# Input statistics of all images taken in the first attention, and new tables for the scan

## The chip, the core and the metric

The kernel runs on one core of a Trainium2 chip. The metric is the device time of one execution in microseconds (us). The core has engines that run their own instruction streams in order and wait for each other on semaphores: TensorE (PE, matmuls and, as PEld, the loads of their weights), VectorE (DVE), ScalarE (ACT), GpSimd (POOL), and SyncE (SP), whose queue issues all the transfers that this document speaks of. Data lies in HBM, in SBUF (on chip, 128 partitions) and in PSUM (where matmuls write).

## What is computed

The input x has 8 images of 256 channels and 48 x 48 = 2304 positions. Two layers are added to it in turn, each behind a group norm (32 groups of 8 channels, so statistics over a whole image are needed before anything else):

```python
def _L0_conv_ref(x, W, bias):          # attention over positions
    tokens = x.reshape(b, c, n).transpose(0, 2, 1)
    feat_pos = tokens @ W.T + bias
    feat, pos = feat_pos[:, :, :c], feat_pos[:, :, c:]
    pos = pos / jnp.maximum(jnp.linalg.norm(pos, axis=-1, keepdims=True), 1e-12)
    sim = jnp.einsum('bnc,bmc->bnm', pos, pos)
    topksim, topkid = jax.lax.top_k(sim, K)            # K = 16
    out = softmax(topksim) weighted sum of feat[topkid]

def step(h, inp):                      # state-space layer, twice in depth
    dA = jnp.exp(dt_t[:, :, None] * A)
    h = h * dA + dt_t[:, :, None] * B_t[:, None, :] * x_t[:, :, None]
    y = jnp.einsum('bds,bs->bd', h, C_t)

x = x + _L0_conv_ref(_gn(x), ...)
x = x + _L1_conv_ref(_gn(x), ...)
```

The second layer is a scan over the 2304 positions with 512 inner channels and 16 states, with a layer norm, an input projection, a convolution of four taps, softplus, a gate (silu of z) and an output projection around it, and all that twice (depth 2).

## The kernel before, in words

**The scan** is the long part. Positions are cut into 6 chunks of T = 384, and each chunk and depth of an image is a *unit*: 12 units an image, 96 in all. A unit has 16 *steps* (32 inner channels with 4 groups of states on 128 partitions, 4 states in each row), and a step has two *parts* of two states each. So a unit has 32 parts and an image 384. The main loop at the end runs over the parts `m` and writes out the order of every engine's work by hand (`manual_schedule`). In each part:

- `decay` on ACT: exp(dt A) for the next part, into one of two PSUM banks (L871);
- `run_scan` on DVE: the scan of the part (L886). `SHARE` says by a letter for each part who multiplies the result by C: with V, DVE does so at once (L888, and ACT's `carry` saves the last column); with G, POOL does it later for the step (`pool_part`, L914), in one instruction of 1536 columns where both parts of the step are G, of 768 where one is;
- at a step's first part, `make_bx` on POOL: the product of B and dt x for a step two ahead (L847), into one of 8 buffers;
- the rows of the tables `between` (ahead of the scan) and `behind` (after it) that fall on this part: loads, projections, norms, `sum_states` (PE sums the states of four steps, L932, and frees their bx buffers), `gate` (DVE, L938), `out_proj` (PE) and `leave` (L967, the residual, DVE; or L963, ACT). A row is (part, function, arguments). Its part counts from the unit's first part, and is negative where it prepares the unit during the one before, so parts over 31 lie in the next unit;
- one step of the generator `layer0` (`ahead.go`).

**The attention** of the first image runs alone before the scan, in pools of its own, under a scheduler that orders the instructions. The attention of image b + 1 runs beside the scan of image b. `layer0` first takes the statistics of the image (`input_stats`, L247: six chunks loaded, bn_stats on DVE, then `group_stats`, a few small operations on DVE, PE, ACT and POOL in turn); then it prepares (`chunk`, `normalized`, `scale`: normalize on ACT, project on PE, norms of pos); then it goes through 18 row blocks of 128 positions, one every 16 parts, by the table `within`: similarities (PE, `similar`; ACT, `keep_similar`), the 16 largest (DVE, `top`, four passes over 2304 columns, L466 to L473), the weights (`others`, `turn`, `weights`), their sum (`weigh`, L516), and the residual (`turn_back`, `finish`, L541), where `average` loads x for one block of 128 positions, `finish` adds and takes bn_stats for the next group norm (L543), and stores x1. `PHASE` and `BLOCK` let the blocks start only at one part in 16.

`layer0` of the first image also takes the statistics of image 1 during its row blocks, one step in every fourth part. For images 2 to 7 the statistics are taken beside the scan, as soon as the image before is done (`Ahead.turn`); in the parts of an image's scan this is from part -42. `SHARE` has three strings: units 1 to 9 of images 0 to 6, which have row blocks beside them; units 0, 10 and 11 of these; and the last image. The tables have two sets: with blocks, and without (`between_spare`, `behind_spare`, chosen by `beside_none`).

Of the kernel before, what the change touches and what calls it, by code (L numbers as in the profile page):

```python
# [1 line left out]

# [13 lines left out]
P = 128  # L16
# [9 lines left out]
def tile_conv_preact(  # L26
# [27 lines left out]
    T = 384  # L54
# [16 lines left out]
    EARLY = -24  # L71
# [3 lines left out]
        "GGVGGGVVGGGGGGVGGGVVGGGVGGGGGVVG",  # L75
        "GVGGVGVVGVVVGVGVGGGGVGVVGVGVGVGV",
        "VGVGVGVGVGVVGGGVGGGVVGVVGVVGGGVG",
# [106 lines left out]
    def group_stats(st, found, mm0, name, more=None):  # L184
# [23 lines left out]
        rstd = small.tile([P, CB], F32, tag="gn_rstd", name=f"rstd_{name}", bufs=4)  # L208
# [5 lines left out]
        shift = small.tile([P, CB], F32, tag="gn_shift", name=f"shift_{name}", bufs=4)  # L214
# [24 lines left out]
    def input_stats(b, pool, mm0, ahead, kept, then=None):  # L239
        bufs = NCH if kept is not None else 3  # L240
        st = small.tile([P, CB, NCH, 6], F32, tag="gn_st0", name=f"st0_{b}")
        xs = {c: load_chunk(pool, x[b], c, "x", f"xs_{b}_{c}", bufs) for c in range(ahead)}
        yield
        for c in range(NCH):
            xt = xs.pop(c)
            for cb in range(CB):
                nc.vector.bn_stats(st[:, cb, c, :], xt[:, cb, :])  # L247
            n = c + ahead
            if n < NCH:
                xs[n] = load_chunk(pool, x[b], n, "x", f"xs_{b}_{n}", bufs)  # L250
            if kept is not None:
                kept[c] = xt
            yield
        found = []
        if then is not None:
            then()
        yield from group_stats(st, found, mm0, f"a{b}")
        known[b] = found

    def layer0(b, left, pool, ps0, alone):  # L260
# [27 lines left out]
        if not alone:  # L288

            def first_chunk():  # L290
                loaded[0] = load_chunk(pool, x[b], 0, "x", f"xt_{b}_0", 3)

            if b in known:
                first_chunk()
                yield
            else:
                yield from input_stats(b, pool, mm0, 2, None, first_chunk)
# [119 lines left out]
        st1 = small.tile([P, CB, NB, 6], F32, tag="gn_st1", name=f"st1_{b}", bufs=1)  # L417
# [102 lines left out]
        def average(t):  # L520
            row = blocks[t]
            row["o"] = pool.tile([P, C], F32, tag="o", name=f"o_{b}_{t}", bufs=more)
            nc.scalar.activation(row["o"], row["po"], AF.Identity, scale=row["den"])
            row["xr"] = pool.tile([P, CB, P], F32, tag="xr", name=f"xr_{b}_{t}", bufs=more)
            nc.sync.dma_start(
                row["xr"], x[b, :, t * P : (t + 1) * P].rearrange("(k p) t -> p k t", p=P)
            )
# [9 lines left out]
        def finish(t):  # L537
            row = blocks[t]
            xr = row["xr"]

            nc.vector.tensor_add(xr, xr, row["pr"].rearrange("p (k t) -> p k t", k=CB))  # L541
            for cb in range(CB):
                nc.vector.bn_stats(st1[:, cb, t, :], xr[:, cb, :])  # L543
            nc.sync.dma_start(x1[:, t * P : (t + 1) * P].rearrange("(k p) t -> p k t", p=P), xr)
# [4 lines left out]
            (21, weights, 3), (4, top, 3), (14, turn, 0), (15, weights, 0), (7, others, 3), (-5, similar, 4),  # L549
            (-8, keep_similar, 0), (-5, keep_similar, 2), (24, turn_back), (18, weigh, 1), (17, weigh, 0),  # L550
            (1, top, 1), (-9, similar, 0), (-8, similar, 1), (-7, similar, 2), (22, average), (-6, similar, 3),
            (-7, keep_similar, 1), (-3, keep_similar, 3), (0, top, 0), (-3, keep_similar, 4), (15, turn, 1),
            (10, others, 4), (5, others, 0), (3, top, 2), (6, add_top), (11, invert), (5, others, 2),
            (17, turn, 2), (20, turn, 3), (15, weights, 1), (18, turn, 4), (18, weights, 2), (21, weigh, 3),
            (7, others, 1), (19, weigh, 2), (20, weights, 4), (21, weigh, 4), (24, finish),
# [7 lines left out]
        other = input_stats(1, pool, mm0, 6, {}) if alone and B > 1 else iter(())  # L563
        for m in range(begin, max(parts) + 1):
            if m >= 0 and m % 4 == 0:
# [389 lines left out]
    def leave(unit, cb):  # L955
# [19 lines left out]
        (-35, center), (7, in_proj, 5), (24, sum_states, 2), (-33, variance), (-21, in_proj, 0),  # L975
        (-15, taps, 1), (37, out_proj, 0), (-15, taps, 2), (-14, taps, 3), (-34, square), (39, leave, 0),
        (23, load_rep, "dt", 14), (5, load_rep, "dt", 5), (-4, load_bc, 1), (38, out_proj, 1), (17, load_d, 2),
        (-17, tap, 1), (18, load_rep, "dtx", 13), (-8, times_x, 1), (19, gate, 1), (-22, normal),
        (1, load_rep, "dt", 3), (0, load_rep, "dtx", 4), (15, load_rep, "dt", 10), (6, load_rep, "dtx", 7),
        (10, load_rep, "dtx", 9), (11, gate, 0), (-29, spread_root), (0, times_x, 3), (-19, load_in, 5),  # L980
        (33, load_out), (8, load_rep, "dtx", 8), (-22, load_in, 0), (21, load_rep, "dt", 13), (-20, tap, 0),
        (-10, step_size, 1), (9, copy_z, 2), (-18, in_proj, 2), (2, load_rep, "dtx", 5), (10, sum_states, 0),
        (13, load_rep, "dt", 9), (29, gate, 2), (9, silu_z), (7, load_rep, "dt", 6), (19, load_rep, "dt", 12),
        (-6, load_rep, "dtx", 1), (-14, load_in, 7), (-30, root), (9, load_rep, "dt", 7), (4, load_d, 1),
        (-24, load_in, 3), (17, load_rep, "dt", 11), (14, load_rep, "dtx", 11), (-13, x_proj),
        (-17, load_in, 6), (-3, load_d, 0), (4, load_rep, "dtx", 6), (-4, load_rep, "dtx", 2), (-42, load_v),
    ]
    behind = [
        (-12, split), (-3, load_rep, "dt", 1), (3, in_proj, 4), (-10, step_size, 0), (-3, load_rep, "dt", 0),
        (-8, load_rep, "dtx", 0), (-15, tap, 3), (-1, load_rep, "dt", 2), (-28, scale),  # L990
        (16, load_rep, "dtx", 12), (11, load_rep, "dt", 8), (8, in_proj, 6), (17, sum_states, 1),
        (-14, silu_x), (28, load_rep, "dt", 15), (-39, affine), (2, times_x, 2), (7, copy_z, 0),
        (19, load_rep, "dtx", 14), (10, load_rep, "dtx", 10), (-17, tap, 2), (-10, softplus),
        (-16, in_proj, 3), (3, load_rep, "dt", 4), (-29, load_in, 2), (6, in_proj, 7), (35, gate, 3),
        (-2, load_rep, "dtx", 3), (8, copy_z, 1), (40, leave, 1), (22, load_rep, "dtx", 15), (-8, load_in, 4),
        (29, load_d, 3), (-37, mean), (-19, taps, 0), (-19, in_proj, 1), (-10, load_bc, 0),
        (33, sum_states, 3), (-30, root_end), (-9, times_x, 0), (-20, load_in, 1),
    ]
    between_spare = [
        (24, sum_states, 2), (-34, variance), (-21, in_proj, 0), (38, out_proj, 0), (-15, taps, 2),  # L1000
        (-14, taps, 3), (-35, square), (39, leave, 0), (20, load_rep, "dt", 14), (5, load_rep, "dt", 5),
        (-4, load_bc, 1), (38, out_proj, 1), (17, load_d, 2), (-17, tap, 1), (18, load_rep, "dtx", 13),
        (-8, times_x, 1), (19, gate, 1), (-22, normal), (9, load_rep, "dtx", 8), (1, load_rep, "dt", 3),
        (0, load_rep, "dtx", 4), (14, load_rep, "dt", 10), (6, load_rep, "dtx", 7), (10, load_rep, "dtx", 9),
        (-18, taps, 0), (12, load_rep, "dtx", 10), (17, load_rep, "dtx", 14), (11, gate, 0), (-1, times_x, 2),
        (-19, load_in, 5), (33, load_out), (-22, load_in, 0), (21, load_rep, "dt", 13), (-20, tap, 0),
        (-10, step_size, 1), (9, copy_z, 2), (-18, in_proj, 2), (2, load_rep, "dtx", 5), (10, sum_states, 0),
        (13, load_rep, "dt", 9), (29, gate, 2), (9, silu_z), (7, load_rep, "dt", 6), (19, load_rep, "dt", 12),
        (-6, load_rep, "dtx", 1), (-14, load_in, 7), (37, gate, 3), (-31, root), (9, load_rep, "dt", 7),
        (5, load_d, 1), (-24, load_in, 3), (17, load_rep, "dt", 11), (14, load_rep, "dtx", 11), (-13, x_proj),  # L1010
        (-17, load_in, 6), (-3, load_d, 0), (4, load_rep, "dtx", 6), (-4, load_rep, "dtx", 2), (-42, load_v),
        (-36, center), (-26, spread_root),
    ]
    behind_spare = [
        (-12, split), (-3, load_rep, "dt", 1), (4, in_proj, 4), (-10, step_size, 0), (-5, load_rep, "dt", 0),
        (-8, times_x, 3), (-8, load_rep, "dtx", 0), (-15, tap, 3), (-1, load_rep, "dt", 2),
# [3 lines left out]
        (-15, taps, 1), (-2, load_rep, "dtx", 3), (8, copy_z, 1), (40, leave, 1), (22, load_rep, "dtx", 15),  # L1020
        (-16, load_in, 4), (29, load_d, 3), (-38, mean), (-21, in_proj, 1), (-12, load_bc, 0),
        (33, sum_states, 3), (-31, root_end), (-9, times_x, 0), (-25, load_in, 1), (-25, scale),
# [3 lines left out]
    def beside_none(m):  # L1026
        image, part = divmod(m, HOOKS * len(order))
        return image + 1 == B or not TOPK[0] * HOOKS <= part < TOPK[1] * HOOKS

    inner, outer = {}, {}  # L1030
    for w, unit in enumerate(units):
        for spare, a, b in ((False, between, behind), (True, between_spare, behind_spare)):
            for table, rows in ((inner, a), (outer, b)):
                for part, f, *args in rows:
                    if spare == beside_none(HOOKS * w + place[f, *args]):
                        table.setdefault(HOOKS * w + part, []).append((f, unit, args))

    class Ahead:
# [16 lines left out]
        def go(self, m):  # L1055
            if self.image == B or m < EARLY:
# [71 lines left out]
```

## Time and profile before

| | |
|---|---|
| time before, median of 3 runs | 9664.73 us (9664.22 to 9666.31) |
| the profiled execution | 9663.76 us, its span 9661.6 us |
| first scan starts | 462.6 us into the span |
| an image's scan, images 0 to 5 | 1167 us |
| last image's scan | 1030 us |
| mean granted clock of TensorE | 0.881 |
| busy, share of the span | PE 83%, DVE 93%, ACT 76%, POOL 92% |

A row of the profile's groups names line, engine, operation, what it writes and reads, shapes and count; then the busy time in us, the mean of one in ns, and the engine's idle time just before such instructions with what ended it. In the chain and the timeline a bracket gives the idle time of the engine ahead of an instruction and who released it. Times in stretches are us from the span's start. The granted clock is the share of TensorE's full speed that the throttle let through.

### The profile page before, as it was taken

The page shows a single profiled execution, that of the slowest core. Times are in us where ns is not written, and L with a number is a line of the kernel's source. Part 1 is how long each engine was busy: PE and PEld are TensorE (multiplying, and loading weights), DVE is VectorE, ACT ScalarE, POOL GpSimd, SP SyncE. Part 2 cuts the span into 40 slices and gives each one's busy share as a digit, 9 for nine tenths or more (in the row PEclk, how much of TensorE's full clock was granted, in tenths as well). Part 3 has the DMA queues.
Part 4 walks back from the last instruction along what each step waited for, and adds up shares of the span by engine and source line. Part 5 has one row for each costly group of instructions (what it writes and reads, how often), then busy time and mean ns, then how long its engine had stood idle before and what let it go on. Part 6 is the DMA issues. An engine that isn't in the chain of part 4 may idle for free. (4 is left out here: it accounts for less than half of the span.)

```text
span 9661.6 us, 120523 instructions
## 1 busy us (share of the span) xinstructions
PE 7986.9 (83%) x36761; PEld 4482.3 (46%) x36761; DVE 8951.2 (93%) x7812; ACT 7303.4 (76%) x16018; POOL 8894.5 (92%) x3983
## 2 busy tenths in 40 slices
PE   8888887888878887888878888788887888866665
PEld 6645544455444554445544555444544455432222
DVE  5599998999989999999999999999999999999998
ACT  4587877777777777777777787777787778777776
POOL 1199999999999999999999999999999999999999
PEclk9989998899979998899988999889998899977777
DMA  1134444434444444444444444444444443444443
GB/s 35 57 126 133 125 142 146 135 126 133 136 152 128 132 131 150 136 131 131 135 146 138 130 128 137 146 138 127 135 128 159 128 133 125 143 138 137 148 146 119
DMA packets 1084999, 1267.54 MB, mean 131 GB/s; under 512 B 109728, under 2 KB 1057440, under 8 KB 1084352
## 3 DMA queue, kind: packets, MB, share of 16 engines
q1 hardware_dynamic: 1083808, 1259.83, 40.8%
q8 instruction: 294, 4.82, 0.2%
q14 instruction: 353, 2.89, 0.1%
q10 hardware_dynamic: 544, 0.00, 0.0%
HBM read 1046.58 MB, written 212.86 MB: 130 GB/s over the span
## 5 line engine op out<-in xcount | busy, mean ns | idle before, releaser
L847 POOL TENSOR_TENSOR bx<-BC,dtxr 128x1536 f32<-128x1536 f32 x1536 | 5302.0, 3458 | 124.5 <-PE y L932 106.4
L871 ACT ACTIVATE da<-dtr,A_sb 128x385 f32<-128x385 f32 x6144 | 3591.6, 585 | 960.0 <-DVE bx L886 703.8
L886 DVE TENSOR_TENSOR_SCAN bx<-da,bx 128x770 f32<-128x770 f32 x1989 | 3428.3, 1746 | 153.7 <-ACT da L871 116.9
L914 POOL TENSOR_TENSOR bx<-bx,BC 128x1536 f32<-128x1536 f32 (+1 forms) x1323 | 3234.8, 2445 | 107.6 <-DVE bx L886 101.1
L886 DVE TENSOR_TENSOR_SCAN da<-da,bx 128x770 f32<-128x770 f32 x1083 | 1899.0, 1753 | 65.0 <-ACT da L871 42.3
L932 PE MATMUL y<-bx,sel 128*32 128x384 f32 x12288 | 1323.5, 539 | 181.4 <-POOL bx L914 160.9
L516 PE MATMUL po<-feat,aT 128*128 128x256 f32 x5184 | 1377.7, 415 | 58.1 <-ACT dt L784 44.1
L645 PE MATMUL pe<-vn,inw 128*128 128x384 f32 (+1 forms) x3072 | 1206.0, 524 | 243.8 <-ACT vn L722 71.7
L445 PE MATMUL psim<-pos 128*128 128x512 f32 x2520 | 1220.6, 620 | 100.0 <-DVE xc L745 78.8
L516 PEld LDWEIGHTS po<-feat,aT 128*128 128x128 f32 x5184 | 1036.8, 207 | 405.3 <-ACT dt L784 114.1
L888 DVE TENSOR_TENSOR bx<-da,BC 128x768 f32<-128x768 f32 x1083 | 1037.6, 958 | 37.3
L932 PEld LDWEIGHTS y<-bx,sel 128*32 128x32 f32 x12288 | 426.0, 118 | 1048.7 <-issue 700.9
L645 PEld LDWEIGHTS pe<-vn,inw 128*128 128x128 f32 x3072 | 577.1, 200 | 707.6 <-issue 117.0
L445 PEld LDWEIGHTS psim<-pos 128*128 128x128 f32 x2520 | 501.7, 212 | 649.3 <-issue 382.0
L745 DVE SCALAR_TENSOR_TENSOR xc<-pe,cw,xc 128x384 f32<-128x384 f32 x1152 | 696.0, 611 | 35.0 <-ACT xc L737 8.0
L505 ACT ACTIVATE aT<-pt 128x512 f32<-128x512 f32 (+1 forms) x720 | 387.3, 548 | 354.7 <-PE pt L497 353.1
L496 PE MATMUL pt<-ident,sim 128*128 128x128 f32 x2592 | 551.5, 291 | 104.0 <-ACT sim L454 57.3
L692 PE MATMUL lv<-ones_mean,lsq 128*128 128x1 f32 x1152 | 233.4, 330 | 477.1 <-ACT lsq L686 477.1
L902 ACT COPY h_st<-da 128x2 f32<-128x2 f32 x878 | 139.8, 159 | 583.9 <-DVE bx L888 581.4
L950 PE MATMUL pw<-z,ow 128*128 128x384 f32 x1536 | 539.4, 498 | 42.3 <-DVE z L938 42.0
L775 PE MATMUL pd<-dbl,dtp_sb 16*128 16x384 f32 x768 | 418.4, 691 | 148.2 <-ACT dbl L768 121.5
L496 PEld LDWEIGHTS pt<-ident,sim 128*128 128x128 f32 x2592 | 379.3, 146 | 277.9 <-ACT sim L454 71.6
(156 smaller groups left out, 10322.3 us busy)
## 6 DMA issues: line engine op xcount, KB each, us to landing
dtxr<-dtx_d SPq DMA_DIRECT2D x1536, 192.0 KB, 2.9
dtr<-dt_d SPq DMA_DIRECT2D x1536, 192.0 KB, 2.8
BC<-bc_d SPq DMA_DIRECT2D x192, 768.0 KB, 5.7
inw<-in_in_wT_dram SPq DMA_DIRECT2D x768, 128.0 KB, 2.5
dtx_d<-dtx SPq DMA_DIRECT2D x384, 192.0 KB, 1.9
dt_d<-dt SPq DMA_DIRECT2D x384, 192.0 KB, 2.1
ow<-in_out_wT_dram SPq DMA_DIRECT2D x96, 512.0 KB, 4.1
dmat<-diag SPq DMA_DIRECT2D x384, 64.0 KB, 3.2
```

The lines of the kernel that those rows point to most:

```text
L445: nc.tensor.matmul(pm, pos[:, k, t * P : (t + 1) * P], pos[:, k, c0 : c0 + w], start=(k == 0), stop=(k == CB - 1),)
L496: nc.tensor.transpose(pt[:, q], row["sim"][:, r], ident)
L516: nc.tensor.matmul(row["po"], aT[:, m % PT, :], feat[:, m, :], start=(m == 0), stop=(m == NB - 1))
L645: nc.tensor.matmul(pe, w[:, k], unit["vn"][:, k, lo:], start=(k == 0), stop=(k == CB - 1))
L745: nc.vector.scalar_tensor_tensor(unit["xc"][e], unit["pe"][e][:, k : k + T], cw[:, unit["d"], e, k : k + 1], unit["xc"][e], ALU.mult, ALU.add,
L847: nc.gpsimd.tensor_tensor(bx[:, :, 1:], unit["BC"][0], unit["dtxr"][i].unsqueeze(1).to_broadcast([P, Q, T]), ALU.mult,)
L871: nc.scalar.activation(da[:, s * (1 + T) : (s + 1) * (1 + T)], unit["dtr"][i], AF.Exp, scale=A_sb[:, unit["d"], i, p * HQ + s : p * HQ + s ...
L886: nc.vector.tensor_tensor_scan(h, da, g, 0.0, ALU.mult, ALU.add)
L888: nc.vector.tensor_tensor(bx[:, :, 0:T], da.rearrange("p (q t) -> p q t", q=HQ)[:, :, 1:], unit["BC"][1][:, qs], ALU.mult,)
L914: nc.gpsimd.tensor_tensor(g[:, :, 0:T], g[:, :, 1:], unit["BC"][1][:, qs], ALU.mult)
L932: nc.tensor.matmul(y[j * G : (j + 1) * G, :], sel, unit["bx"][k * J + j][:, q, 0:T], start=False, stop=True, skip_group_check=True,)
L950: nc.tensor.matmul(pw, unit["ow"][:, k, cb * P : (cb + 1) * P], unit["z"][k], start=(k == 0), stop=(k == DB - 1),)
```

## The change

The statistics of all images are taken during the first attention: `input_stats` of images 1 to 7 run one after the other, one step in every second part, and `layer0` beside the scan only loads its first chunk. The statistics' tile moves to the attention's pool, and the small tiles that keep the results (`gn_rstd`, `gn_shift`) get 16 buffers. The preparation beside a scan does not start before a fixed part, `EARLY` = -21 of that scan. `average` loads x for three blocks at once (a chunk of 384 columns), `finish` takes bn_stats and stores x1 once for three. `SHARE` is new in all three strings. The tables are new, with `within` changed in places (the first `top` a part sooner, `weigh` 2 a part later, `weigh` 0 and `weights` 4 a part sooner, `invert` a part later), and the last image has a set of its own, which holds the same rows as that for units 0, 10 and 11.

```diff
-    EARLY = -24
+    EARLY = -21
...
-        "GGVGGGVVGGGGGGVGGGVVGGGVGGGGGVVG",
-        "GVGGVGVVGVVVGVGVGGGGVGVVGVGVGVGV",
-        "VGVGVGVGVGVVGGGVGGGVVGVVGVVGGGVG",
+        "GGVGGGVGGGVVGGVGGGGVGGGVGGGGGVVG",
+        "GVGGGGVVGGVVGGGVVGGGVGVVGVGVGVGV",
+        "VVVGVVGGVGVVGGGVGGGVGGVVGVVGGGVG",
...
-        rstd = small.tile([P, CB], F32, tag="gn_rstd", name=f"rstd_{name}", bufs=4)
+        rstd = small.tile([P, CB], F32, tag="gn_rstd", name=f"rstd_{name}", bufs=2 * B)
...
-    def input_stats(b, pool, mm0, ahead, kept, then=None):
-        bufs = NCH if kept is not None else 3
-        st = small.tile([P, CB, NCH, 6], F32, tag="gn_st0", name=f"st0_{b}")
+    def input_stats(b, pool, mm0, ahead, kept):
+        st = pool.tile([P, CB, NCH, 6], F32, tag="gn_st0", name=f"st0_{b}", bufs=2)
...
-            if b in known:
-                first_chunk()
-                yield
-            else:
-                yield from input_stats(b, pool, mm0, 2, None, first_chunk)
+            first_chunk()
+            yield
...
-            row["xr"] = pool.tile([P, CB, P], F32, tag="xr", name=f"xr_{b}_{t}", bufs=more)
-            nc.sync.dma_start(
-                row["xr"], x[b, :, t * P : (t + 1) * P].rearrange("(k p) t -> p k t", p=P)
-            )
+            if t % TB == 0:
+                tag, bufs = ("xr", 2) if alone else ("x", 3)
+                rows[t // TB] = load_chunk(pool, x[b], t // TB, tag, f"xr_{b}_{t}", bufs)
...
+            c, j = divmod(t, TB)
+            xr = rows[c][:, :, j * P : (j + 1) * P]
             nc.vector.tensor_add(xr, xr, row["pr"].rearrange("p (k t) -> p k t", k=CB))
-            for cb in range(CB):
-                nc.vector.bn_stats(st1[:, cb, t, :], xr[:, cb, :])
-            nc.sync.dma_start(x1[:, t * P : (t + 1) * P].rearrange("(k p) t -> p k t", p=P), xr)
+            if j + 1 == TB:
+                xr = rows.pop(c)
+                for cb in range(CB):
+                    nc.vector.bn_stats(st1[:, cb, c, :], xr[:, cb, :])
+                nc.sync.dma_start(x1[:, c * T : (c + 1) * T].rearrange("(k p) t -> p k t", p=P), xr)
...
-        other = input_stats(1, pool, mm0, 6, {}) if alone and B > 1 else iter(())
+        other = iter(())
+        if alone:
+            other = chain.from_iterable(input_stats(o, pool, mm0, 6, {}) for o in range(1, B))
         for m in range(begin, max(parts) + 1):
-            if m >= 0 and m % 4 == 0:
+            if m >= 0 and m % 2 == 0:
                 next(other, 0)
...
-            if self.image == B or m < EARLY:
+            if self.image == B or m < EARLY + (self.image - 1) * HOOKS * len(order):
                 return
```

Of the tables with blocks beside them, the rows that move, as (part before, part after): `leave` 1 (40, 38), `copy_z` 1 (behind 8, between 8), `sum_states` 2 (24, 25), `sum_states` 3 (behind 33, between 32), `gate` 1 (19, 21), `gate` 2 (between 29, behind 29), `square` (between -34, behind -35), `times_x` 3 (0, -3), `in_proj` 7 (6, 5), `load_in` 1 (behind -20, between -21), `load_d` 1 (between 4, behind 5), `load_rep` dt 0 (behind -3, between -3). Of those without blocks: `sum_states` 2 (24, 25), `gate` 2 (29, 31), `taps` 3 (between -14, behind -14), `center` (between -36, behind -37), `spread_root` (-26, -29), `scale` (-25, -28), `load_rep` dtx 9 (10, 11), dt 14 (20, 23), dt 0 (behind -5, between -5), dt 2 (behind -1, between -1), `load_d` 3 (behind 29, between 29).

## The prediction

> **What bounds the kernel now.** I read the page first, then the busy time by unit of the scan, then the waits inside one unit, then the same few microseconds engine by engine. Sections 1 and 5 of the page:
>
> ```profile
> PE 7986.9 (83%) x36761; PEld 4482.3 (46%) x36761; DVE 8951.2 (93%) x7812; ACT 7303.4 (76%) x16018; POOL 8894.5 (92%) x3983
> ...
> L847 POOL TENSOR_TENSOR bx<-BC,dtxr 128x1536 f32<-128x1536 f32 x1536 | 5302.0, 3458 | 124.5 <-PE y L932 106.4
> L888 DVE TENSOR_TENSOR bx<-da,BC 128x768 f32<-128x768 f32 x1083 | 1037.6, 958 | 37.3
> ```
>
> VectorE (DVE) and GpSimd (POOL) are both almost full. SHARE hands each half step's product with C either to DVE (V, 0.958 us) or to POOL (G, 1.69 us alone, 3.19 us as a pair GG). So a unit cannot be much shorter than POOL's busy time in it, and what can be won is idle time of these two. The table by stretch has one row per unit of image 2 (its scan starts at 2797.0): units 0, 1, 4, 5, 10, 11, then units 10 and 11 of image 6, beside which nothing is prepared, then a unit of the last image. Columns are length, busy PE, PEld, DVE, ACT, POOL, granted clock, DMA.
>
> ```profile
> 2797.00:2890.80 93.80, 72.78 (x328) 39.76 (x328) 84.81 (x76) 71.67 (x155) 87.80 (x62) 0.83 0.43 138
> 2890.80:2986.80 96.00, 78.58 (x339) 40.63 (x337) 93.62 (x78) 75.15 (x170) 95.00 (x35) 0.89 0.39 126
> 3183.50:3283.30 99.80, 87.85 (x411) 50.38 (x411) 95.56 (x84) 78.19 (x175) 94.96 (x35) 0.91 0.42 131
> 3283.30:3380.40 97.10, 87.16 (x412) 50.01 (x413) 94.62 (x82) 77.61 (x175) 94.97 (x35) 0.92 0.41 131
> 3771.60:3871.00 99.40, 67.57 (x315) 34.23 (x318) 89.76 (x93) 67.26 (x155) 90.59 (x46) 0.77 0.52 170
> 3871.00:3964.40 93.40, 77.06 (x347) 44.51 (x348) 82.95 (x74) 77.32 (x160) 85.03 (x58) 0.88 0.45 143
> 8441.10:8532.70 91.60, 65.18 (x306) 33.17 (x306) 83.86 (x79) 67.21 (x154) 82.84 (x42) 0.82 0.43 140
> 8532.70:8618.50 85.80, 55.91 (x225) 24.11 (x224) 80.90 (x72) 60.27 (x116) 85.80 (x37) 0.74 0.45 146
> 9051.40:9136.90 85.50, 58.55 (x224) 24.57 (x226) 78.80 (x68) 63.55 (x146) 85.50 (x35) 0.76 0.43 142
> ```
>
> Read them as POOL's busy time plus its idle time. Units 1 and 5 waste 1 to 2 us. Units 3, 4 and 6 (99.9, 99.8, 99.2) waste over 4. Units 10, 11 and 0 waste 8.8, 8.4 and 6.0. The last image wastes nothing: POOL is the bound. The sums over an image: units 1 to 9 take 880.8 us, of which POOL works 855.4; units 0, 10 and 11 take 286.6, of which it works 263.4.
>
> Two causes can be named. The waits of unit 10:
>
> ```profile
> DVE st L247 <- DMA xs<-in_x_dram: 5.0, 1, 5.0
> POOL bx L914 <- DVE bx L886: 5.3, 1, 5.3
> ```
>
> The first bn_stats of the next image stands in DVE's order one part after its load was issued, DVE stops for the landing, and POOL stops behind DVE. The other cause, in unit 4, in order of time on PE, POOL and DVE:
>
> ```profile
> 3210.44 1.82 PE L645 MATMUL pe<-vn,inw 128*128 128x384 f32 x4 [1.88 <-DVE xr L967]
> 3212.05 3.36 PE L516 MATMUL po<-feat,aT 128*128 128x256 f32 x8
> ...
> 3215.59 1.95 PE L516 MATMUL po<-feat,aT 128*128 128x256 f32 x8
> ...
> 3218.11 2.79 PE L932 MATMUL y<-bx,sel 128*32 128x384 f32 x32
> ...
> 3220.96 3.46 POOL L847 TENSOR_TENSOR bx<-BC,dtxr 128x1536 f32<-128x1536 f32 x1 [4.75 <-PE y L932]
> ...
> 3221.12 0.56 DVE L938 TENSOR_TENSOR z<-y,z 128x384 f32<-128x384 f32 x1 [2.44 <-PE y L932]
> ```
>
> PE waits 1.88 us for a PSUM buffer that `leave` (L967) frees only at part 8 of the next unit, then works off two `weigh` calls, and `sum_states(0)` comes late: the gate on DVE waits 2.44 us and POOL 4.75 us, since its next bx buffer is freed by that sum. Units 3, 6, 8 and 10 show the same place.
>
> **The change part by part.**
>
> *Statistics out of the scan* (images 2 to 7). Per image 6 loads on SP's queue, 12 bn_stats (L247, 0.544 us) and 2 aggregates on DVE, 10 small POOL operations (0.2 us each), 4 on ACT and 2 matmuls leave unit 10. DVE loses 6.5 us of work and the wait (31.5 us over all of L247, 5.0 of it at the kernel's start, so 26.5/6 = 4.4 each).
>
> *Preparation from part -21.* It began at -42 with 15 parts of statistics, so the projections move about 7 parts later, out of unit 11 into unit 0: the same instructions, 0, with bounds of 2 us either way (27 parts of preparation cost unit 11 93.4 - 85.8 = 7.6 us against image 6; 7/27 of that is 2.0). What waits behind it is `similar` of block 0, one part after the preparation now ends instead of eight; its late chunks are needed only three parts on.
>
> *Row blocks.* By the code, preparation ended at part 21 and waited for part 28; now it ends at 28. The first maximum of block 0 comes at part 37 instead of 38. So the blocks do not move by 16 parts against this kernel, and I give that nothing.
>
> *SHARE of units 0, 10, 11.* V falls from 16 to 14, pairs GG rise from 3 to 5, single G fall from 10 to 8: POOL +2 x 3.19 - 2 x 1.69 = +3.0 us a unit, DVE -2 x 0.96 = -1.9. Nothing hides 3 us on POOL when it is the bound. Summed with the two items above for one image: POOL's work 263.4 - 2.0 + 9.0 = 270.4. Its idle time was 23.2: 6.4 of it is the stall of unit 10 (5.3 and 1.1 behind it), 4.0 are gate waits at part 10; 12.8 remain (7.7 of it POOL waiting for ACT's root), and a fuller POOL meets them later, so 8 to 13. That gives 278 to 283, taken at 281: -5.6 us x 6 images = -34. Image 6 has no preparation and POOL full in unit 11 (85.80 of 85.80): +3 there, -2 in unit 10: -33 in all. Bounds: -11 an image (idle falls to 5) to +4 (idle stays at 20).
>
> *Stage with blocks (63 units).* SHARE keeps 9 V, one GG becomes two singles: 2 x 1.69 - 3.19 = +0.2 us on POOL, 9 an image +1.8. `leave(1)` goes from part 40 to 38 (frees the buffer before the wait above), `weigh(2)` from behind part 9 to behind part 10, after `sum_states(0)`; each `weigh` is 1.9 us of PE. `square` goes from part 30 to 29, so the 3.60 us that PE waits at part 30 (lv L692 <- ACT lsq L686) shrinks. `sum_states(3)` goes one part up: it now waits on PE for POOL's last product of the unit, with `similar(3)` and `(4)` queued behind; in unit 5 that product was done at 3286.0 and PE, without the wait at part 30, would come there at about 3281 to 3284, so 2 to 5 us of PE wait, about the 3.6 saved. POOL's 25.4 idle us of units 1 to 9 are 12.4 around part 10 and 9.9 at part 22 (DVE behind with its taps and two V; one of these V is moved to the unit's first half). I take two thirds of the first and four tenths of the second, 8 + 4 us, minus 1.8: -10.2 an image, x 7 = -71. Bounds: +13 (only the longer POOL work) to -148 (all idle of both places gone).
>
> *x in chunks, and its statistics.* Loads and stores of the row blocks fall from 144 to 48 each on SP's queue; bn_stats from 36 of 0.285 (starts 0.24 apart) to 12 of 0.544 an image, 2.2 us less on DVE, but 1.1 in one go every third block. DVE is not alone the bound there: 0, counted in the two thirds above. The x buffers are shared by three users; a row's chunk lives 36 parts of 48, `res` 8, so none waits.
>
> *Load rows* (dt 0, 2 and 14, dtx 9, d 1 and 3, in 1) move by three parts at most on SP's queue; such a load lands in 2.5 to 3.2 us, about one part, and is used three or more parts later: 0; one part of wait each, 3 us a unit, if the queue held them up.
>
> *Last image (12 units).* SHARE 3 GG + 11 G becomes 5 + 7: 5 x 3.19 + 7 x 1.69 - 3 x 3.19 - 11 x 1.69 = -0.4 us x 12 = -4.6; POOL is the bound, so -4 (0 to -10).
>
> *First attention.* It takes the 72 bn_stats (39 us of DVE), 36 loads (SP's queue issues 5 loads in 32 to 40 us and nothing more until 106) and the small steps. PE is the bound there (47 of every 50 us, DVE 31), and DVE's four passes wait 4 to 5 us for `sim` in each block, which hides the statistics. Before the first maximum at 75.3 us, 60 bn_stats now stand in DVE's order instead of 24; the 18 chunks that are new there follow image 1's at about 43 us and, at 1.9 us each (the kernel's first six are in by 11.2), are in by about 77. I take +4: 2 there and 2 for the larger last chunk between attention and scan. Bounds: 0 to +65 (39 of work and 26 of waits, all on the path).
>
> Sum: -33 - 71 - 4 + 4 = -104. The profiled execution took 9663.8 (span 9661.6 and 2.2 around it), 1.0 below the median of 9664.7: 9560.7, said as 9560.
>
> **The rivals.**
>
> *The stage with blocks wins nothing* (the waits go elsewhere: gate 1, gate 2, `similar` behind `sum_states(3)`). For it: two engines at 98% leave little room. Against it: the named wait has a named cause that moves. -104 + 71 = -33: 9632.
>
> *All idle of the two places goes*, and units 0, 10, 11 reach their bound: -11 x 6 for these, -110 for the blocks (halfway to their bound), -6 for the rest: -182: 9480.
>
> *First attention pays in full*: -104 + 61 = -43: 9622. For it: DVE waited 4.4 us for each image's first load. Against: there the loads run well ahead.
>
> *Slower: TensorE at half clock before gate 0.* Between 3211.6 and 3218.4 the granted clock is 0.75 in the row of that stretch, and a `weigh` takes 3.36 us instead of 1.89, just ahead of `sum_states(0)`. Units 3, 4 and 6 are hit and are 2.7 us longer than 5 and 7. If the changed order puts such a stretch there in all nine units, 6 more are hit: 6 x 2.7 x 7 = +113 in place of -71: 9745. It decides from about two more units an image (33 / 18.9 = 1.7): then the gain is gone. [...]
>
> **How the numbers follow.** Forecast 0.42, more won 0.12, nothing in the block stage 0.20, first attention 0.10, slower 0.13, no change 0.03. What a measurement of this kernel can tell from no change is 0.2%, 19 us. The range 9470 to 9665 leaves out the slower case and the far end of the best one. Faster 0.83, same 0.04, slower 0.13.
>
> **What would show it.** Right: no wait of L247 on a load after the first attention; units 10 at 90 to 92; no gate wait over 1 us at part 10 of units 4 and 6, and units 3, 4 and 6 at 96 to 98; the first scan at about 466 instead of 462.6; units of the last image 0.4 us shorter. Wrong: POOL idle over 20 us in units 0, 10, 11 together; a granted clock near 0.75 before gate 0 in more units; `keep_similar` on ACT waiting over 2 us at part 3; the first scan after 480.

## The result and the profile after

The changed kernel takes 9635.4 us (median of 8 runs, 9631.1 to 9637.0) against 9663.1 for the kernel before (8 runs, 9661.3 to 9666.3). The ratio is 0.9971, 95% interval 0.9962 to 0.9980: 28 us less. The forecast was 104 us less. The sign is right and the time lies inside the range, but three quarters of the forecast gain are missing. The profiled execution's span is 9633.4 us, 28.2 shorter than that of before.

Sections 1 and 5 of the changed kernel's page, the lines that answer to those shown of before:

```profile
PE 7912.8 (82%) x36761; PEld 4383.1 (45%) x36761; DVE 8925.0 (93%) x7578; ACT 7298.4 (76%) x16026; POOL 8959.6 (93%) x4022
...
L845 POOL TENSOR_TENSOR bx<-BC,dtxr 128x1536 f32<-128x1536 f32 x1536 | 5304.4, 3458 | 29.5 <-PE y L930 25.1
...
L886 DVE TENSOR_TENSOR bx<-da,BC 128x768 f32<-128x768 f32 x1041 | 997.6, 958 | 35.8
```

DVE has 40 us less of its product, POOL 65 us more work. POOL's wait for PE's sums in front of its big product fell from 106.4 to 25.1 us, as forecast. The same stretches as before the change, with the same columns (length, busy PE, PEld, DVE, ACT, POOL, clock, DMA): units 0, 1, 4, 5, 10, 11 of image 2, units 10 and 11 of image 6, a unit of the last image.

```profile
2788.50:2885.60 97.10, 80.19 (x357) 44.66 (x357) 83.71 (x75) 74.44 (x161) 92.05 (x68) 0.85 0.44 141
2885.60:2981.50 95.90, 78.29 (x341) 40.40 (x340) 93.09 (x76) 75.33 (x171) 93.86 (x36) 0.91 0.39 127
3173.80:3273.50 99.70, 86.30 (x411) 48.22 (x410) 95.70 (x83) 77.98 (x177) 95.32 (x36) 0.93 0.42 135
3273.50:3370.50 97.00, 86.96 (x412) 48.68 (x411) 94.55 (x80) 77.67 (x177) 96.06 (x36) 0.92 0.41 129
3758.30:3855.40 97.10, 66.05 (x306) 33.70 (x304) 88.39 (x77) 67.08 (x152) 87.78 (x43) 0.76 0.41 137
3855.40:3952.50 97.10, 75.07 (x320) 40.62 (x319) 80.23 (x71) 73.60 (x148) 91.47 (x48) 0.82 0.46 151
8414.10:8511.20 97.10, 65.76 (x305) 33.74 (x304) 88.27 (x77) 67.09 (x152) 87.79 (x43) 0.76 0.41 136
8511.20:8600.50 89.30, 57.54 (x226) 24.57 (x224) 79.18 (x70) 60.33 (x116) 88.50 (x38) 0.77 0.43 141
8943.90:9029.20 85.30, 56.65 (x224) 24.24 (x226) 79.92 (x70) 63.51 (x143) 85.30 (x33) 0.80 0.45 147
```

Unit 4 is as long as before (99.8, now 99.7). Unit 10 is 97.1, where 90 to 92 was forecast, and its POOL is idle for 9.3 us. Image 6 has nothing prepared beside it and its unit 10 is just as long, so that loss does not come from the preparation. Added up over the kernel:

| part | forecast, us | measured, us |
|---|---|---|
| units 1 to 9, seven images | -71 | 872.7 against 880.8, -8.1 x 7 = -57 |
| units 0, 10, 11, images 0 to 5 | -34 | 291.1 against 286.6, +4.5 x 6 = +27 |
| units 0, 10, 11, image 6 | +1 | 283.4 against 271.1, +12 |
| last image | -4 | 1020.2 against 1029.6, -9 |
| first attention | +4 | scan starts at 462.05 instead of 462.57, -0.5 |
| sum | -104 | -28 |

Units 0, 10 and 11 miss their forecast by 72 us, of 76 in all. The timeline of unit 10 of image 2 in the changed kernel shows one cause: start, duration, engine, line, what it writes and reads, and in brackets the idle time ahead. First DVE, then POOL:

```profile
3802.22 0.48 DVE L190 BATCH_NORM_AGGREGATE mv_b<-st 128x2 f32<-128x36 f32 x2
3802.74 7.12 DVE L192 TENSOR_TENSOR mv_b<-mv_b,b_feat 128x2 f32<-128x2 f32 x1
3809.77 1.76 DVE L884 TENSOR_TENSOR_SCAN da<-da,bx 128x770 f32<-128x770 f32 x1
```

```profile
3801.37 3.46 POOL L845 TENSOR_TENSOR bx<-BC,dtxr 128x1536 f32<-128x1536 f32 x1
3804.78 1.69 POOL L912 TENSOR_TENSOR bx<-bx,BC 128x768 f32<-128x768 f32 x1
3806.41 3.42 POOL L845 TENSOR_TENSOR bx<-BC,dtxr 128x1536 f32<-128x1536 f32 x1
3816.16 1.68 POOL L912 TENSOR_TENSOR bx<-bx,BC 128x768 f32<-128x768 f32 x1 [6.33 <-DVE bx L884]
```

`group_stats` adds the bias to two means per partition: 128x2 elements, 7.12 us. The addition ends at 3809.86, with a POOL product (3806.41 + 3.42 = 3809.83). Two others stand back to back ahead of that one, and the addition, which started during the first of the three, ran on through all of them. DVE's scans wait behind it, and POOL, which needs them, then stands idle for 6.33 us. All instances of this instruction in one row (count, then shortest, median and longest in ns, then first and last start), in the changed kernel:

```profile
L192 DVE TENSOR_TENSOR mv_b<-mv_b,b_feat x8: 160/7115/7142, 401.8 to 8458.5; 128x2 f32<-128x2 f32 x8
```

and in the kernel before:

```profile
L191 DVE TENSOR_TENSOR mv_b<-mv_b,b_feat x8: 161/1166/1191, 403.2 to 8488.2; 128x2 f32<-128x2 f32 x8
```

The one short instance is that of the first attention (start 401.84 us), where POOL is idle for 44.73 us up to 402.78. The other seven stand in unit 10 of images 0 to 6, and in both kernels each of them ends within 0.03 us of the end of a POOL product behind which POOL pauses. In before, the addition started during the last product ahead of that pause. The rows of unit 10, on DVE and POOL:

```profile
3818.70 1.16 DVE L191 TENSOR_TENSOR mv_b<-mv_b,b_feat 128x2 f32<-128x2 f32 x1
...
3816.41 3.43 POOL L847 TENSOR_TENSOR bx<-BC,dtxr 128x1536 f32<-128x1536 f32 x1
3825.15 3.18 POOL L914 TENSOR_TENSOR bx<-bx,BC 128x1536 f32<-128x1536 f32 x1 [5.31 <-DVE bx L886]
```

3816.41 + 3.43 = 3819.84, and 3818.70 + 1.16 = 3819.86. So there the addition ended with the product that ran when it started, and POOL paused for 5.31 us behind it; with the new share two more products followed without a pause.

The second loss is in the stage with blocks. The list of waits, in the order engine, line, releaser, us in total, times, longest; the changed kernel:

```profile
POOL bx L912 <- DVE bx L884: 179.4, 121, 6.3
...
DVE z L936 <- PE y L930: 67.0, 32, 6.6
...
DVE xr L965 <- PE pw L948: 37.7, 23, 2.4
```

and the kernel before:

```profile
DVE z L938 <- PE y L932: 125.2, 75, 7.9
...
POOL bx L914 <- DVE bx L886: 101.1, 96, 5.3
...
DVE xr L967 <- PE pw L950: 4.4, 3, 2.2
```

The gate's wait for the sums is halved. A wait of `leave` (L965) for `out_proj` (L948) is new, up to 2.4 us, and POOL waits 78 us more for DVE's scans, 70 of them in units 1 to 9 (118.9 for 48.7). In the same units the gate's waits for PE's sums (54.6 us) and POOL's (72.3) are gone altogether. In unit 4 of the changed kernel, DVE:

```profile
3194.23 1.14 DVE L965 SCALAR_TENSOR_TENSOR xr<-pw,b_feat,xr 128x384 f32<-128x384 f32 x2 [2.38 <-PE pw L948]
```

`leave(1)` at part 38 stands right behind `out_proj(1)` of the same part, so DVE stops until PE's last eight matmuls of it are done.

### The profile page after: what moved, and what is told of

It reads as the page before. It is cut to its first block, busy times and chain, and to the rows that moved or that the text cites. A ratio compares the mean times of both kernels' runs of the same rounds, so it can differ in the third digit from the quotient of the medians.

```text
span 9633.4 us, 120225 instructions
## 1 busy us (share of the span) xinstructions
PE 7912.8 (82%) x36761; PEld 4383.1 (45%) x36761; DVE 8925.0 (93%) x7578; ACT 7298.4 (76%) x16026; POOL 8959.6 (93%) x4022
## 5 line engine op out<-in xcount | busy, mean ns | idle before, releaser
L845 POOL TENSOR_TENSOR bx<-BC,dtxr 128x1536 f32<-128x1536 f32 x1536 | 5304.4, 3458 | 29.5 <-PE y L930 25.1
L884 DVE TENSOR_TENSOR_SCAN bx<-da,bx 128x770 f32<-128x770 f32 x2031 | 3507.0, 1747 | 221.6 <-ACT da L869 161.3
L912 POOL TENSOR_TENSOR bx<-bx,BC 128x768 f32<-128x768 f32 (+1 forms) x1362 | 3302.9, 2425 | 180.8 <-DVE bx L884 179.4
L884 DVE TENSOR_TENSOR_SCAN da<-da,bx 128x770 f32<-128x770 f32 x1041 | 1824.6, 1753 | 73.5 <-ACT da L869 53.1
L930 PE MATMUL y<-bx,sel 128*32 128x384 f32 x12288 | 1345.9, 547 | 209.1 <-POOL bx L912 189.7
L440 PE MATMUL psim<-pos 128*128 128x512 f32 x2520 | 1198.9, 611 | 182.7 <-DVE xr L535 79.2
L886 DVE TENSOR_TENSOR bx<-da,BC 128x768 f32<-128x768 f32 x1041 | 997.6, 958 | 35.8
L440 PEld LDWEIGHTS psim<-pos 128*128 128x128 f32 x2520 | 479.4, 203 | 694.0 <-issue 348.3
L948 PE MATMUL pw<-z,ow 128*128 128x384 f32 x1536 | 531.4, 493 | 40.2 <-ACT aT L500 38.4
L927 PE MATMUL y<-xc,dmat 128*128 128x384 f32 x768 | 419.3, 635 | 115.4 <-ACT h_st L922 27.3
L483 ACT ACTIVATE rest<-left,three 128x512 bf16<-128x512 f32 (+1 forms) x720 | 453.2, 668 | 68.2 <-DVE left L468 68.2
L492 PE MATMUL pt<-minus,rest 128*128 128x128 bf16 x2592 | 494.0, 225 | 7.3 <-ACT rest L483 7.3
```

The lines of the kernel that those rows point to most:

```text
L440: nc.tensor.matmul(pm, pos[:, k, t * P : (t + 1) * P], pos[:, k, c0 : c0 + w], start=(k == 0), stop=(k == CB - 1),)
L845: nc.gpsimd.tensor_tensor(bx[:, :, 1:], unit["BC"][0], unit["dtxr"][i].unsqueeze(1).to_broadcast([P, Q, T]), ALU.mult,)
L884: nc.vector.tensor_tensor_scan(h, da, g, 0.0, ALU.mult, ALU.add)
L886: nc.vector.tensor_tensor(bx[:, :, 0:T], da.rearrange("p (q t) -> p q t", q=HQ)[:, :, 1:], unit["BC"][1][:, qs], ALU.mult,)
L912: nc.gpsimd.tensor_tensor(g[:, :, 0:T], g[:, :, 1:], unit["BC"][1][:, qs], ALU.mult)
L930: nc.tensor.matmul(y[j * G : (j + 1) * G, :], sel, unit["bx"][k * J + j][:, q, 0:T], start=False, stop=True, skip_group_check=True,)
```

## The experiments

All of them compute the whole output. Ratios are to the kernel before, with 95% intervals.

**1. The addition with one SBUF input.** The bias goes in as a per-partition scalar:

```diff
-            nc.vector.tensor_add(mv[:, :, 0], mv[:, :, 0], more)
+            for cb in range(CB):
+                nc.vector.tensor_scalar(
+                    mv[:, cb, 0:1], mv[:, cb, 0:1], more[:, cb : cb + 1], None, ALU.add
+                )
```

> Base: the changed kernel. The addition of b_feat to the means of the row-block statistics (128x2, once an image, 7.12 us in the scan, 0.16 us in the first attention) is written as two additions with a per-partition scalar, so that it reads one SBUF tensor in place of two. Port theory: the two-input form cannot run while POOL works without a pause (it ends with POOL's third product, 3809.83 against 3809.86); each of the new ones takes under 0.3 us, POOL's 6.3 us wait in unit 10 goes, unit 10 falls from 97.0 to about 91, the kernel by 7 x 6 = 42 us to about 9593. Rival, data: the addition waits for the aggregates or for its tile; the same 7 us, the same time, 9635. Rival, POOL: the wait goes but POOL is full anyway; a gain of 20 us or less.

Measured: 9588.5 us, 0.9924 (0.9911 to 0.9936), 46.9 less than the changed kernel, near the 42 that were expected. All instances in one row, and unit 10 of image 2:

```profile
L193 DVE TENSOR_SCALAR mv_b<-mv_b,b_feat x16: 153/186/215, 401.9 to 8417.8; 128x1 f32<-128x1 f32 x16
```

```profile
3745.30:3835.90 90.60, 64.63 (x307) 33.43 (x306) 81.42 (x77) 67.14 (x153) 87.91 (x43) 0.82 0.45 147
```

It takes 0.33 us for two, beside the same busy POOL, and unit 10 falls from 97.1 to 90.6. By durations alone, 7 x (7.12 - 0.33) = 47.5 us; the time fell by 46.9. The whole length of this one instruction lies on the path. The edit changes the operation and the shape together with the number of whole tiles read from SBUF (the scalar lies there too). That the operation alone does not do it is seen on the product by C (L886), which is also a TENSOR_TENSOR but reads one of its inputs from PSUM, beside the same POOL; all its instances in the changed kernel:

```profile
L886 DVE TENSOR_TENSOR bx<-da,BC x1041: 957/958/962, 467.0 to 9617.6; 128x768 f32<-128x768 f32 x174
```

**2. The old share of products in units 0, 10 and 11**, with the long form of the addition left in:

```diff
-        "GVGGGGVVGGVVGGGVVGGGVGVVGVGVGVGV",
+        "GVGGVGVVGVVVGVGVGGGGVGVVGVGVGVGV",
```

> Base: the changed kernel, with the SHARE string of units 0, 10 and 11 as before (16 V for 14). Share theory: POOL sets these units, so it gives back 3.0 us in each of 21 units, 63 us, and the addition finds POOL's old pauses (1.2 us for 7.1), 42 us less: together 9530 to 9560. Rival: units 0 and 11 are set by the preparation's chain over PE and ACT, and only the addition counts: about 9593. Rival: DVE becomes late by its 1.9 us a unit: 9620 or more.

Measured: 9568.8 us, 0.9902 (0.9889 to 0.9916), 66.6 less than the changed kernel; 75 to 105 less was expected. The addition, untouched in its code, is short again:

```profile
L192 DVE TENSOR_TENSOR mv_b<-mv_b,b_feat x8: 161/1271/1469, 402.0 to 8399.0; 128x2 f32<-128x2 f32 x8
```

So its median went from 7.12 to 1.27 us by POOL's share of products alone.

**3. Both.** The two edits together.

> Both edits of the two runs before. If port and share are each a cause, the addition counts once: within 10 us of the old SHARE alone, 9530 to 9555, and below the one-input form alone by about 60. If SHARE costs nothing, the same as the one-input form alone.

Measured: 9557.5 us, 0.9892 (0.9877 to 0.9907). Against experiment 1 the old share is worth another 31.0 us, about 60 was expected. That is 1.5 us in each of the 21 units, half of the 3.0 of added POOL work that the prediction counted. In units 0, 10 and 11 of images 0 to 5 POOL's work falls from 271.2 to 262.2 us on average, as counted, but its idle time rises from 13.0 to 18.4: the fuller POOL had met part of these waits later, as the prediction said. Against experiment 2 the short addition is worth 11.3 us, not 46.9: most of its price is paid only beside the new share.

**4. The input statistics alone.** On the kernel before: the statistics of all images in the first attention and the preparation from part -21, with shares, tables and x loads untouched. The lines of the edit that are not shown move the statistics' tile to the attention's pool and give the small tiles more buffers.

```diff
-    EARLY = -24
+    EARLY = -21
...
-            if b in known:
-                first_chunk()
-                yield
-            else:
-                yield from input_stats(b, pool, mm0, 2, None, first_chunk)
+            first_chunk()
+            yield
...
-        other = input_stats(1, pool, mm0, 6, {}) if alone and B > 1 else iter(())
+        other = iter(())
+        if alone:
+            other = chain.from_iterable(input_stats(o, pool, mm0, 6, {}) for o in range(1, B))
...
-            if m >= 0 and m % 4 == 0:
+            if m >= 0 and m % 2 == 0:
...
-            if self.image == B or m < EARLY:
+            if self.image == B or m < EARLY + (self.image - 1) * HOOKS * len(order):
```

> Base: the kernel before, with the statistics of all images in the first attention and the preparation from part -21, nothing else (row blocks start as before; SHARE, tables and x in pieces as before). If the statistics were worth in unit 10 what the comparison with image 6 shows (99.3 to 91.6), 6 x 7.6 = 46 us less: about 9617, with units 0 and 11 together unchanged. Rival: preparation in unit 0 costs what unit 10 saves: 9650 to 9663.

Measured: 9601.6 us, 0.9937 (0.9923 to 0.9950), 61.6 less than before; 46 less was expected. This one part is worth more than twice what the whole change brought. Units 0, 10 and 11 of image 2:

```profile
2773.80:2868.90 95.10, 78.70 (x365) 44.76 (x366) 85.63 (x76) 75.73 (x166) 87.46 (x67) 0.86 0.44 140
3748.60:3840.20 91.60, 65.16 (x306) 33.08 (x306) 83.85 (x79) 67.22 (x154) 82.84 (x42) 0.82 0.43 140
3840.20:3930.90 90.70, 69.67 (x311) 38.75 (x310) 81.96 (x73) 72.42 (x146) 89.67 (x48) 0.84 0.49 162
```

Together they take 277.4 us instead of 286.6: -9.2.

**5. Units 0, 10 and 11 with their old tables too**, on experiment 3. The core of the edit, as rows and not as lines of code (`taps` 3, `center` and the load rows `dt` 0, 2, 14, `dtx` 9 and `d` 3 go back as well; the last image keeps its new set):

```diff
-(25, sum_states, 2)  (31, gate, 2)  (-29, spread_root)  (-28, scale)
+(24, sum_states, 2)  (29, gate, 2)  (-26, spread_root)  (-25, scale)
```

> Base: one-input addition and the old SHARE string of units 0, 10 and 11 (9557.5), and besides the two tables of these units (rows without blocks) as before; those of the last image stay new. With the statistics moved alone, these three units took 277.6 us an image against 281 to 283 here. Table theory: the new rows cost the difference, about 4.5 us an image: 30 us less, about 9528. Rival: the difference comes from how the units with blocks hand over, and the time stays at 9557.

Measured: 9539.6 us, 0.9873 (0.9858 to 0.9887), 17.9 less than experiment 3; 30 less was expected. So three new things cost time in these units: the long addition, the share and the rows.

**6. `leave` 1 one part later**, at 39, on experiment 5:

```diff
-(38, leave, 1)
+(39, leave, 1)
```

> Base: the run with old tables in units 0, 10 and 11; the residual's second half (leave 1) beside blocks one part later, at 39 for 38. At 38 it stands right behind out_proj 1 and DVE waits for it 2.4, 1.0 and 1.5 us in units 4, 6 and 8. Theory: one part later the wait goes, and these units lose up to that: 10 to 30 us less. Rival, buffer theory: PE waits for the PSUM buffer again, the gate at part 11 comes late, and the time is equal or longer.

Measured: 9495.4 us, 0.9827 (0.9812 to 0.9841), 44.2 less than experiment 5, where 10 to 30 was expected, and 168 less than before: the best kernel of this study. Its waits:

```profile
POOL bx L915 <- DVE bx L887: 115.9, 81, 4.4
...
DVE xr L968 <- PE pw L951: 4.2, 2, 2.2
...
POOL bx L848 <- PE y L933: 7.9, 7, 1.2
```

and unit 4 of image 2, where DVE no longer waits for `out_proj`:

```profile
3133.50:3230.50 97.00, 84.67 (x411) 48.34 (x410) 95.50 (x83) 78.35 (x177) 95.28 (x36) 0.94 0.43 139
```

In the changed kernel unit 4 took 99.7. In units 1 to 9 of an image POOL's idle time was 25.4 us before (880.8 - 855.4), is 17.7 in the changed kernel (872.7 - 855.0) and 11.3 here (867.5 - 856.2). `leave` at 39 still frees the PSUM buffer in time: POOL's wait for `sum_states` does not come back.

**7. `leave` 1 at part 40**, as it was in the kernel before, with all else of experiment 5 (the edit of experiment 6 with 40).

> Same base; leave 1 beside blocks at 40, as in the kernel before. Buffer theory (the prediction's): PE waits 1.9 us at part 9, gate 0 waits 2.4 us and POOL 4.7 us again in units 4 and 6: 3 us each there, 2 in unit 3: 35 to 55 us more. Rival, order theory: the moved weigh already keeps the sum early, so nothing comes back: within 10 us of the base, or less where DVE's new wait goes.

Measured: 9557.6 us, 0.9889 (0.9875 to 0.9904): 18 slower than at 38 and 62 slower than at 39. Expected were the old waits and 35 to 55 us more than at 38, or, by the rival, no more than 10. The wait of `leave` is gone here too, so that wait alone does not explain the order of the three. Nor did the old gate wait of over 1 us return in units 4 and 6. What is new is this row of the list of waits:

```profile
PE pt L494 <- DVE xr L968: 43.7, 21, 3.1
```

PE's turning of the weights (L494) waits for the buffer that `leave` frees. The kernel before, with `leave` at 40 and the attention's old rows, has no such wait on PE, nor have experiments 5 and 6. So in the new order the buffer is wanted earlier (which of the moved rows does that was not tried), and the useful place for `leave` lies between 38, where it waits for `out_proj`, and 40, where PE waits for it. Whether these 43.7 us are the whole of the 62 was not tried.

**8. The share of the stage with blocks as before**, on experiment 5:

```diff
-        "GGVGGGVGGGVVGGVGGGGVGGGVGGGGGVVG",
+        "GGVGGGVVGGGGGGVGGGVVGGGVGGGGGVVG",
```

> Same base, with the SHARE string of the units with blocks as before (9 V both, 0.2 us less on POOL a unit, two neighbouring V at parts 18 and 19 and at 6 and 7 instead of 10 and 11). Theory that the string only moves POOL's wait from part 22 to part 17: within 10 us of the base. Theory that it carries the gain of these units (8 us an image): 40 to 57 us more.

Measured: 9540.3 us, 0.9872 (0.9856 to 0.9889), 0.7 from experiment 5. This string carries nothing that can be measured here.

**9. Three of the attention's rows as before**, on experiment 6 (again as rows):

```diff
-(20, weigh, 2)  (16, weigh, 0)  (19, weights, 4)
+(19, weigh, 2)  (17, weigh, 0)  (20, weights, 4)
```

> Base: the run with leave 1 at 39 (9495.4). weigh 0, weigh 2 and weights 4 go back to their parts in the kernel before (17, 19, 20). Order theory: the sum of the first four steps comes late again, gate 0 and POOL's next product wait for it at parts 10 and 11, as in the kernel before (2.4 and 4.7 us in units 4 and 6): 20 to 60 us more. Rival: the earlier leave already frees PE there, and the time stays within 10 us.

Measured: 9511.5 us, 0.9845 (0.9831 to 0.9858), 16 slower than experiment 6, between the 20 to 60 that were expected and the 10 of the rival. The loss is not in the stage with blocks: units 1 to 9 take 867.5 us an image on average, as in experiment 6 (867.3), and the gate's and POOL's waits for the sums do not come back there. It is in units 0, 10 and 11: 277.7 us for 275.7 in images 0 to 5, 274.7 for 270.9 in image 6. With one of the two edits alone, the new rows (experiment 7) or the earlier `leave` (this one), these waits stay away from units 1 to 9, beside the rest of the change. Why the rows matter in units 0, 10 and 11 was not tried.

**10. The changed kernel with `leave` 1 at 39** and nothing else (the edit of experiment 6).

> Base: the changed kernel as it is; leave 1 beside blocks at 39 for 38, nothing else. If DVE's wait for out_proj 1 is a cost by itself, the same as between the two runs with that edit: 40 to 50 us less, 9585 to 9595. Rival: beside the long addition and the fuller POOL of units 0, 10 and 11 it is hidden: 20 us less or nothing.

Measured: 9581.4 us, 0.9916 (0.9902 to 0.9929): 54 less than the changed kernel, where 40 to 50 was expected. The effect does not depend on the repairs in units 0, 10 and 11.

The runs make a ladder from the kernel before to the changed one, each step a difference of two medians: statistics and preparation alone -61.6; blocks, chunks, last image and the short addition -62.0 (experiment 4 to 5); new rows of units 0, 10, 11 +17.9 (5 to 3); their new share +31.0 (3 to 1); the long addition +46.9 (1 to the changed kernel). The steps add up to the measured -27.7 because each starts where the one before ends, so the sum is no check; and another order would split it otherwise (with the old share back first, the share is 66.6 and the addition 11.3).

## Why the prediction was right and wrong

**Where it failed: units 0, 10 and 11, -33 forecast, +39 measured.** The step that failed is the one on POOL's idle time: "12.8 remain ..., and a fuller POOL meets them later, so 8 to 13". Measured in image 2 are 20.0 us (97.10 - 92.05, 97.10 - 87.78, 97.10 - 91.47). POOL's work was sized well, 271.3 us for 270.4. What was missed is that work of DVE takes longer beside the fuller POOL (the addition's median is 7.12 us for 1.17): the addition appears nowhere in the sum, and beside the new share it costs 47 us. Without it (experiment 1) POOL's idle time in these units is 13.2 us, at the end of the stated range. Its old row was within reach: 1.17 us for an instruction that takes 0.16 when POOL is idle, with an end 0.02 us from that of a POOL product. Experiments 1 and 2 show this cause from both sides, by the form of the instruction and by what POOL does beside it. As two tiles the addition took 7.12 us, with the bias as a scalar 0.19 a column (medians). In the changed kernel it lasted not to the end of the POOL product that ran when it started (3804.83 us), but to that of the third in a row (3809.83). What of the chip the two engines share there no run shows: "port" in the expectations of experiments 1 and 3 stands for these durations.

**Unit 10's wait was misread, and the size held by luck.** The prediction put POOL's 5.31 us down to DVE's wait for the statistics' load. That POOL wait ends at 3825.2, while the load's wait ends at DVE's first bn_stats at 3846.5, 21 us later, and POOL works on without a pause beside it. In front of POOL's wait, DVE works on the block statistics, the addition and the taps (L745). In unit 10 of experiment 4, which has no input statistics, the wait is still there:

```profile
POOL bx L910 <- DVE bx L882: 5.3, 1, 5.3
```

POOL is idle for 8.8 us in unit 10 in both kernels (99.40 - 90.59 and 91.60 - 82.84), and the prediction's own table has the same 8.8 in unit 10 of image 6, which has no statistics beside it either. Experiment 4 won 9.2 us in units 0, 10 and 11 of image 2, where 6.4 of idle time and 2.0 of POOL work had been credited. It won them elsewhere: POOL's work fell by 3.5 us, its idle time in unit 11 fell from 8.4 to 1.0, and that in unit 0 rose by 1.6.

**Moved preparation and rows.** In experiment 4 unit 11 lost 2.7 us (93.4 to 90.7) and unit 0 gained 1.3 (93.8 to 95.1); the bounds were 2 either way. The moved rows of units 0, 10 and 11 were put at nothing; experiment 5 measured 17.9 us for them, 2.6 an image over seven images. Which row it is was not tried.

**The stage with blocks, -71 forecast, -57 measured.** The mechanism held as far as the named waits go: the gate's and POOL's waits for the sums are gone from units 1 to 9, and units 3 and 6 are 3.8 and 2.2 us shorter. Of 25.4 idle us of POOL the forecast left 13.4, and 17.7 stayed. The missed step is the other end of "`leave(1)` goes from part 40 to 38": the prediction asked whom it frees and not what it waits for, and `out_proj(1)` is of that same part. Experiments 6 and 10 measured 44 and 54 us for this; part 38 is still 18 us better than the old 40 (experiment 7). `sum_states(3)` one part up was put at nothing net, and no run tries it alone: over the whole kernel PE's wait for POOL's products in front of all `sum_states` went from 160.9 to 189.7 us, its wait for `square` from 477.1 to 226.2. The lower bound of -148 does not follow from its terms, which give (12.4 + 9.9 - 1.8) x 7 = 144; nothing rests on it.

**Smaller terms.** The first attention hides the statistics entirely (-0.5, forecast +4): DVE's work in the first 462 us rose from 239.7 to 270.1, PE's stayed at 405 to 408. The last image gained 9 instead of 4. Counted to the end of the trace it is 10.1 us: 4.6 of it is POOL's work, as summed, and 5.5 is POOL's idle time, which the prediction had put at nothing. No wait on a statistics load was left in the scans.

**The rivals.** "The stage with blocks wins nothing" gave 9632, 3 us from the result, and is false: that stage won 57. "First attention pays in full" did not occur. The half clock did not spread. In slices of one part each (unit length / 32, image 2), the granted clock of units 3, 4 and 6 fell to 0.56, 0.51 and 0.66 within parts 7 to 9 in before, and is 1.00 there now; in part 23 it is 0.50 in all three in both kernels, and in part 31 it lies between 0.50 and 0.72. Unit 4's granted clock rose from 0.91 to 0.93. What brings such a hit on, no run shows. The price that the slower rival put on a hit was misread too. In before, the first parts of unit 3 have the hit in image 2 and not in image 3; parts 5 to 10 of the two:

```profile
3096.47:3116.08 19.61, 16.62 (x69) 11.37 (x67) 17.79 (x12) 11.58 (x25) 19.11 (x10) 0.91 0.45 141
4264.20:4283.81 19.61, 16.62 (x74) 11.29 (x72) 17.79 (x12) 11.59 (x25) 19.12 (x10) 1.00 0.45 141
```

Both stretches take 19.61 us and both units 99.9, so what unit 3 takes more than unit 5 does not come from this hit. In units 4 and 6 every image has it, and no such pair can be set side by side.

## What to carry to other kernels

Where GpSimd is made fuller, look on VectorE's timeline for small instructions that last far longer than the same instruction elsewhere and end with a GpSimd product. Here it was an addition of two SBUF tiles, 7.12 us for 0.16, and the list of waits shows no wait of VectorE for it. With the second operand as a per-partition scalar it took 0.19 us a column; where that operand is one, try the same. An operation moved up in a fixed order has two ends: name what it frees and what it will then wait for, and try the place between.

## What the runs showed of the hardware

A VectorE addition of 128x2 elements with both inputs in SBUF took 0.16 us with GpSimd idle, 1.17 us when it met the end of one GpSimd product, and 7.12 us when three products ran back to back; it ended at none of the boundaries between them (3804.8 and 3806.4 us), but at 3809.86. With the bias as a per-partition scalar the same sum took 0.15 to 0.22 us for each of its two columns; in unit 10 of image 2 both, 0.33 us together, ran inside one GpSimd product (3787.99 to 3791.44 us). The product by C, the same kind of instruction with one input in PSUM, took 0.957 to 0.962 us in all its 1041 instances, in a kernel whose GpSimd is busy for 93% of the span. The profile counts the addition's whole length as busy time of VectorE: unit 10's DVE shows 88.39 us busy with the long form and 81.42 with the short one.
